# A graph network of two layers on one core: a channel kept as a row, and loads, a sum and a product moved to later places in their queues

## The chip, the core and the metric

The kernel runs on one core of a Trainium2 chip. A core has a matrix engine (TensorE, PE in the profile), a vector engine (VectorE, DVE), a scalar engine (ScalarE, ACT), a general engine (GpSimd, POOL) and a synchronising engine (SyncE, SP) that here only issues DMAs. Each engine works through its own queue in order and waits on semaphores for the others. The metric is the device time of one execution in microseconds; the median of three runs before the change is 2042.75 us (2042.57 to 2043.82).

## What is computed

64 graphs of N = 256 nodes with D = 256 channels go through two layers, all in fp32. Cut to what matters:

```python
# layer 0
h = einsum(d^-1/2 A d^-1/2 + alpha I, x)      # A: adjacency, d: degrees
x = layernorm(x + h @ W.T + b)                # this x is called x1 in the kernel
# layer 1
h = relu(bn1(conv1(x)))                       # 1 tap
x_conv = relu(bn2(conv2(h)) + x)              # 17 taps along the nodes, 256 x 256 channels
s = x @ w_se.T + b_se                         # 3 numbers a node
A = exp(-|s_n - s_m|^2);  msg = relu(x @ w_msg.T + b_msg);  x_nmp = A @ msg
out = GRU(input=[x_conv, x_nmp], state=x)     # w_ih (3D x 2D), w_hh (3D x D)
x = layernorm(x + out)
```

## The kernel before

**Rounds.** The 64 graphs go in NQ = 4 rounds of Q = 16. For each graph, `layer0` makes x1 and stores it to DRAM (L461); `layer1` transposes it (`x1_transposed`, L464), runs conv1 (L487), the messages (L508), a transform of h along the nodes (L526) into the tile V, the distances and their exponentials (L550, L551), the weighing by the adjacency (L554) and the aggregation (L563), and stores the transposed x1 and x_nmp to DRAM as xn_d (L568). The 17-tap convolution is done for a whole round at once: products of V with transformed weights u (`products`, L611, loads of u on SP at L581, six tiles deep), then an inverse transform on DVE (`complex_end`, L787) which stores to DRAM as xc_d.

**Gates.** The GRU of a graph (`gru`, L914) follows a round later. It is done as seven products instead of eight by a Strassen-like scheme: p1 to p7, each three matmuls (six records in the profile) of 128 x 384, with sums of blocks of the input made on POOL (`input_sums`, L893, line L901) and sums of weights in the tile wall made once in the first round (`gate_weights`, L1156). The first four gates of a round (EARLY = 4) are spread among the last graphs of the next round; the other twelve run beside the next round's products; the sixteen gates of the last round run alone at the end. `in_blocks(g)` is true for the first four of each round and all of the last: 28 graphs.

**Early gates' input.** For these 28, x_conv's argument is loaded in blocks (L830), transposed on DVE (L872, or L874 in the last round), x1 is added to it on POOL (L875), and two ReLUs on ACT follow (L879). Layer 1 folds the biases into the matmuls through channel 0: `x1_transposed` writes a constant 1 in place of it (L471, with `unit` and `others_only`), so the transposed tile lacks channel 0 of x1. That channel is loaded apart, as a column of x1_d with 256 elements of 4 bytes each (L844), into a tile of one partition, and added to partition 0 on POOL (L876); one is taken off again in the ReLU's bias (`less_one`).

**Queues and order.** The code is a set of generators; each `yield` is a place where another one may go on, and `graphs` (L1083), `merge`, `take` and `paced` say in what order they are written. That order is a priority only: a scheduler then goes through each engine's work, and takes a later instruction first where an earlier one is not ready by its own estimate of times. What must not move ahead is held by `with tc.issue_after(i):`, which puts what the block holds behind instruction `i` in the same engine's queue, without a wait. In the first round, `others` (L1193) gives each graph i one part of the transformed weights: `weights(setup, i, scale2)` (L316), 13 parts with matmuls, a difference on DVE (L339), a sum on POOL (L340) and three stores issued by POOL (L342); the graphs 13 to 15 have the gate weights' steps instead. `load_x` and `load_adj` (L108, L104) fetch the graph three ahead, on SP. `load_gate`, `load_conv` and `load_x1` (L838, L823, L846) fetch a gate's data, on SP too.

In a gate, the order of the products is this (a is the part of the input, b the part of wall):

```python
        p1 = product(A11, B11)          # evicted to `first` by ACT, L941
        p7 = product(S[3], T3)
        ...
        p6 = product(S[2], T2)          # the sixth product
        mark(nc.vector.tensor_add(quarter(0, 1), first, p6), 1)          # L947
        nc.vector.tensor_add(quarter(1, 1), quarter(0, 1), p7)           # L948
        product(A12, B21, p1)
        ...
        p5 = product(S[1], T1)
        ...
        product(A22, T4, p7)            # onto p7, so behind L948
        ...
        product(S[4], B22, p5)
```

The products lie in four banks of PSUM. After them come tanh (L977, L993), the mixing on DVE (L983 to L995) and the last layernorm (L353 to L364, with a power on POOL at L356).

Of the kernel before, what the change touches and what calls it, by code (L numbers as in the profile page):

```python
# [26 lines left out]
def kernel(  # L27
# [79 lines left out]

    def load_x(g):  # L108
        xin[g] = loads.tile([P, NCH, D], F32, name="x_t")
        nc.sync.dma_start(xin[g], x[g].rearrange("(c p) f -> p c f", p=P))  # L110

    def load(g):
        if g < B:
# [9 lines left out]

    vectors = const.tile([16, P], F32, name="bn_in")
    unused = const.tile([P, N], F32, name="unused")
    neg_half = const.tile([P, 4], F32)
    nc.vector.memset(neg_half, -0.5)
    load(0)
# [241 lines left out]

    xc_d = [dram.tile([Q, N, D], F32, name=f"xc_d{q}") for q in range(NQ)]
    x1_d = [dram.tile([Q, N, D], F32, name=f"x1_d{q}") for q in range(NQ)]
    xn_d = [dram.tile([P, 2 * DCH, N], F32, name=f"xn_d{g}") for g in range(B)]
    XN = {}
    ALONE = set()
    EXP, WEIGHED, NORMED = {}, {}, []
    gate = None
    EAGER = {0, Q - 4, Q - 3, Q - 2, *range(Q, Q + 13), 2 * Q + 5, 2 * Q + 6, 3 * Q + 5, 3 * Q + 6}
# [85 lines left out]
    def x1_transposed(g):  # L464
        x1 = X1.pop(g)
        xn = XN[g] = work.tile([P, 2 * DCH, N], F32, name="xn")
        p = bank("p_x1T").rearrange("p (k n) -> p k n", k=DCH)
        for k in range(DCH):
            for c in range(NCH):
                nc.tensor.transpose(p[:, k, c * P : (c + 1) * P], x1[:, c, k * P : (k + 1) * P], ident)  # L470
        nc.scalar.activation(xn[:, 0], p[:, 0], AF.Identity, bias=unit, scale=others_only)  # L471
        nc.scalar.copy(xn[:, 2 * DCH - 1], p[:, 1])

    def layer1(g, place):

# [8 lines left out]
        for c in range(NCH):  # L484
            p = bank("p_conv1")[:, : D + NSE]
            for k in range(DCH):
                nc.tensor.matmul(  # L487
                    p, x1T[:, k, c * P : (c + 1) * P], wc1[:, k, :], start=k == 0, stop=k == DCH - 1
                )
# [86 lines left out]

    TILES, AWAY = [V], []

    def load_u(n, i):
        u = ustream.tile([P, DCH, D], F32, name="u")  # L580
        nc.sync.dma_start(  # L581
            u, ud[i][n * GC : (n + 1) * GC].rearrange("c g o -> (c g) o")[:D].rearrange("(p k) o -> p k o", k=DCH)
        )
        return u

    def product(p, j, v, u, onto=False):
# [227 lines left out]

    GATE, CONV, SUMS, OWN, CHANNEL = {}, {}, {}, {}, {}


    EARLY = 4

    def in_blocks(g):  # L820
        return g % Q < EARLY or g >= B - Q

    def load_conv(g):  # L823
        y = xc_d[g // Q][g % Q]
        if in_blocks(g):


            CONV[g] = gate.tile([P, DCH, N // RB, RB], F32, name="xc_blocks", tag="xc_g")
            for b in range(NB):
                nc.sync.dma_start(  # L830
                    CONV[g][b * RB : (b + 1) * RB],
                    y.rearrange("(s r) (k b j) -> b r k s j", r=RB, k=DCH, j=RB)[b],
                )
            return
        CONV[g] = gate.tile([P, NCH, D], F32, name="xc_g")
        nc.sync.dma_start(CONV[g], y.rearrange("(c p) d -> p c d", p=P))

    def load_gate(g):  # L838
        inputs = GATE[g] = gate.tile([P, 3 * DCH, N], F32, name="inputs")
        nc.sync.dma_start(inputs[:, : 2 * DCH], xn_d[g])  # L840
        if in_blocks(g):
            CHANNEL[g] = gate.tile([1, N], F32, name="channel", bufs=1)
            with nc.allow_non_contiguous_dma("one channel"):
                nc.sync.dma_start(CHANNEL[g], x1_d[g // Q][g % Q][:, 0:1].rearrange("n d -> d n"))  # L844

    def load_x1(g):  # L846
        OWN[g] = gate.tile([P, NCH, D], F32, name="x1_g")
        nc.sync.dma_start(OWN[g], x1_d[g // Q][g % Q].rearrange("(c p) d -> p c d", p=P))

    def sent(g):  # L850

# [12 lines left out]
    def transposed(g):  # L864

        inputs = GATE[g]
        xcT = inputs[:, 2 * DCH :]
        if in_blocks(g):
            to = xcT.rearrange("p k (s r) -> p k s r", r=RB)
            if g < B - Q:  # L870
                with tc.issue_after(WEIGHED[max(WEIGHED)]):
                    nc.vector.transpose(to, CONV.pop(g))  # L872
            else:
                behind(nc.vector.transpose(to, CONV.pop(g)))  # L874
            nc.gpsimd.tensor_tensor(xcT, xcT, inputs[:, 0 : 2 * DCH : 2 * DCH - 1], op=ALU.add)  # L875
            JOINED.append(nc.gpsimd.tensor_tensor(xcT[0:1, 0], xcT[0:1, 0], CHANNEL.pop(g), op=ALU.add).ins)  # L876
            with tc.issue_after(EXP[max(EXP)]):
                for k in range(DCH):
                    nc.scalar.activation(xcT[:, k], xcT[:, k], AF.Relu, bias=less_one[:, k : k + 1])  # L879
# [34 lines left out]
    def gru(g):  # L914
# [33 lines left out]
        nc.vector.tensor_add(quarter(1, 1), quarter(0, 1), p7)  # L948
        product(A12, B21, p1)
# [84 lines left out]
    def chain(*stages):  # L1034
        for stage in stages:
            yield from stage
# [37 lines left out]
    PLACES = (("other",), ("layer0",), ("layer0",), (), ("layer0",), ("other", "layer0"), ())  # L1074
    STATS, APPLIED = len(PLACES) - 1, 1
    ENDS = [iter(())]

    def of_layer0(g):
        if g not in LAYER0:
# [3 lines left out]
    def graphs(first, part, others):  # L1083


        for i in part:
# [7 lines left out]
            for piece, _ in enumerate(layer1(first + i, i)):  # L1094
                if piece == APPLIED:
                    with tc.issue_after(EVICTED[first + i]):
                        run(ENDS.pop())
                    ENDS.append(given["layer0"])
                elif piece == STATS:
                    next(given["layer0"], "end")  # L1100
                    next(of_layer0(first + i + 3), "end")
                    next(given["layer0"], "end")
                if AWAY and TILES[0] is V:
                    g = first + i
                    if g >= 2 * Q:
                        if piece == 5:
                            bring(g, nc.scalar.copy, 1, EXP[g])
                    elif piece == 2:
                        bring(g, nc.vector.tensor_copy, 4, DIAGONAL[g + 2])
                    elif piece == 5:  # L1110
                        bring(g, nc.scalar.copy, 3, EXP[g])
                        bring(g, nc.vector.tensor_copy, 5, WEIGHED[g])
                yield
                for name in PLACES[piece]:
                    if next(given[name], "end") != "end":
                        yield
                if piece == 0 and not first:
                    with tc.issue_after(TAPS_OF["last"]):
                        load_x(i + 3)
            yield from given["other"]  # L1120

    with tc.tile_pool(name="setup", bufs=1) as setup:
# [30 lines left out]
        without_first(wmsg, top[:, D + NSE :], nc.gpsimd)  # L1153
        nc.gpsimd.tensor_copy(wmsg[0:1, 0], biases[:, NSE:])

        def gate_weights():  # L1156
            for b, i, h in ((B11, 0, 0), (T1, 0, 1), (B21, 1, 0), (B22, 1, 1)):
                at = slice(h * HD, (h + 1) * HD)
                own = w_hhT[i * P : (i + 1) * P].rearrange("p (t d) -> p t d", t=3)
                nc.sync.dma_start(wall[:, b, 0, 0:1], own[:, 2:3, at])  # L1160
                nc.sync.dma_start(wall[:, b, 0, 1:3], own[:, 0:2, at])
                for k in range(DCH):
                    row = (D if i == 0 else 0) + k * P
                    nc.sync.dma_start(
                        wall[:, b, 1 + k], w_ihT[row : row + P].rearrange("p (t d) -> p t d", t=3)[:, :, at]
                    )
            nc.gpsimd.tensor_copy(less_one, bn2_bias)
            nc.gpsimd.tensor_tensor(less_one[:, 0:1], less_one[:, 0:1], unit, op=ALU.subtract)
            top = setup.tile([P, 3, 2, HD], F32, name="hh_top", tag="taps", bufs=2)
# [185 lines left out]
```

## Time and profile before

| | us |
|---|---|
| median of three runs | 2042.75 |
| profiled execution, whole | 2048.04 |
| its span | 2046.3 |
| VectorE busy in it | 1396.4 |
| ScalarE busy in it | 964.7 |
| GpSimd busy in it | 698.1 |
| mean clock granted to TensorE | 0.994 |

The profile is one execution, taken with the hardware profiler. A row of a timeline gives the start from the beginning of the span, the duration, the engine, the line of the kernel, the operation, the tiles (written <- read) and the shapes; in brackets stands how long the engine had been idle before it and what ended that wait. Matmuls are pipelined: a record of 128 x 384 is 0.49 us long, but the next one starts 0.32 us after it, so a bracket of 0.2 hides another 0.17. A row of the chain of waits gives start, duration and what the end of the execution was waiting for at that time. SPq and ACTq rows are issues of DMAs; their duration is that of the issue, not of the transfer. DMA engines are busy 33.8% of the span for SP's queue, 9.3% for ACT's and 6.3% for POOL's.

The first round takes the span up to about 256 us, its products come then; the products of the later rounds begin near 600, 1089 and 1571 us, and the last sixteen gates run alone from about 1800 us on.

### The profile page before, as it was taken

To read this page: it belongs to the slowest core of one execution; us is meant where nothing else is said; L and a number is where in the kernel's file an instruction comes from. 1 tells how busy PE (TensorE), PEld (TensorE's weight loads), DVE (VectorE), ACT (ScalarE), POOL (GpSimd) and SP (SyncE) were. 2 spreads that over 40 slices of the span, in tenths; PEclk is the share of its full clock that TensorE was granted. 3 is DMA by queue.
4 is the path that set the end of the run, shared out by engine and by line. 5 is a ranking of instruction groups with operands and counts; after the bars stand their busy time and mean duration, and the time that the engine had idled before them with its cause. 6 is when DMAs were issued, how large, how long until landed. Compare 5 with 4: busy or idle time off the path is not lost. (4 is left out here: it accounts for less than half of the span.)

```text
span 2046.3 us, 26391 instructions
## 1 busy us (share of the span) xinstructions
PE 1984.9 (97%) x8157; PEld 1437.7 (70%) x8157; DVE 1396.4 (68%) x3199; ACT 964.7 (47%) x2285; POOL 698.1 (34%) x679
## 2 busy tenths in 40 slices
PE   7999999999999999999999999999999999999997
PEld 6878788878667766777777766777777855555554
DVE  6334447787567788764546888874445899877787
ACT  5666654567442234566653233556664233333333
POOL 4444411232532143223322234322331045445543
PEclk8999999999999999999999999999999999999999
DMA  4766557544555654343336665334344745443431
GB/s 133 221 202 207 182 193 240 169 140 135 138 149 192 212 126 134 115 129 109 103 109 185 211 170 134 119 117 125 97 116 142 259 124 135 127 100 87 102 87 54
DMA packets 269021, 298.05 MB, mean 146 GB/s; under 512 B 84276, under 2 KB 211336, under 8 KB 268882
## 3 DMA queue, kind: packets, MB, share of 16 engines
q1 hardware_dynamic: 208842, 200.37, 33.8%
q10 hardware_dynamic: 44472, 67.39, 9.3%
q0 software_dynamic: 15568, 28.62, 6.3%
q8 instruction: 66, 1.08, 0.2%
q14 instruction: 73, 0.60, 0.1%
HBM read 193.19 MB, written 103.06 MB: 145 GB/s over the span
## 5 line engine op out<-in xcount | busy, mean ns | idle before, releaser
L930 PE MATMUL p_g<-wall,sums 128*128 128x384 f32 x1536 | 534.0, 488 | 6.1 <-POOL sums L901 3.2
L930 PEld LDWEIGHTS p_g<-wall,sums 128*128 128x128 f32 x1536 | 284.8, 190 | 193.4 <-issue 9.6
L930 PE MATMUL p_g<-wall,inputs 128*128 128x384 f32 x1152 | 406.8, 489 | 12.2 <-DVE G L948 12.2
L930 PEld LDWEIGHTS p_g<-wall,inputs 128*128 128x128 f32 x1152 | 215.3, 190 | 167.2 <-DVE G L948 27.8
L356 POOL TENSOR_TENSOR ln_rs<-ln_rs,neg_half 128x2 f32<-128x2 f32 x129 | 95.2, 738 | 546.7 <-DVE ln_rs L355 411.0
L901 POOL TENSOR_TENSOR sums<-inputs 128x384 f32<-128x384 f32 x128 | 143.1, 1118 | 329.0 <-PE p_g L930 303.2
L554 DVE TENSOR_TENSOR aT<-aT,adjT 128x512 f32<-128x512 f32 x64 | 45.2, 706 | 200.5 <-ACT aT L551 200.4
L435 POOL TENSOR_TENSOR x_t<-x_t,b_t 128x512 f32<-128x512 f32 x64 | 101.9, 1592 | 215.3 <-ACT x L432 138.8
L589 PE MATMUL p_k<-u,VM 128*128 128x256 f32 x736 | 169.6, 380 | 2.8 <-DMA u<-ud 1.6
L589 PEld LDWEIGHTS p_k<-u,VM 128*128 128x128 f32 x736 | 138.5, 190 | 25.6 <-PE p_k L589 2.5
L364 ACT ACTIVATE x_g<-x_g,ln_mr,ln_rs 128x256 f32<-128x256 f32 x128 | 70.0, 593 | 169.4 <-DVE ln_mr L360 164.6
L977 ACT ACTIVATE G<-G 128x512 f32<-128x512 f32 (+1 forms) x129 | 81.0, 628 | 128.7 <-DVE G L1004 91.9
L440 PE MATMUL p_hT<-adjT,x 128*128 128x256 f32 x512 | 125.7, 389 | 5.8 <-ACT x L432 2.3
L487 PE MATMUL p_conv<-wc,xn 128*128 128x259 f32 x512 | 126.5, 389 | 4.2 <-ACT xn L471 3.5
L563 PE MATMUL p_nmp<-aT,msg 128*128 128x256 f32 x512 | 121.4, 380 | 2.2 <-DVE aT L554 2.2
L450 PE MATMUL p_out<-w,hT 128*128 128x256 f32 x512 | 121.5, 380 | 0.9 <-ACT hT L445 0.7
L901 POOL TENSOR_TENSOR sums<-inputs,sums 128x384 f32<-128x384 f32 x64 | 74.8, 1169 | 138.0 <-PE p_g L930 137.9
L508 PE MATMUL p_msg<-wmsg,xn 128*128 128x256 f32 x512 | 121.9, 381 | 0.0
L487 PEld LDWEIGHTS p_conv<-wc,xn 128*128 128x128 f32 x512 | 99.1, 194 | 27.1 <-ACT xn L471 4.3
L526 PE MATMUL p_dft<-fwd,h 128*128 128x240 f32 x512 | 114.1, 366 | 0.0
L950 ACT COPY G<-p_g 128x512 f32<-128x512 f32 x64 | 37.4, 584 | 155.9 <-PE p_g L930 107.2
L450 PEld LDWEIGHTS p_out<-w,hT 128*128 128x128 f32 x512 | 95.6, 190 | 21.2 <-ACT hT L445 2.9
(173 smaller groups left out, 3596.9 us busy)
## 6 DMA issues: line engine op xcount, KB each, us to landing
u<-ud SPq DMA_DIRECT2D x284, 256.0 KB
xn_d<-xn ACTq DMA_DIRECT2D x64, 512.0 KB
inputs<-xn_d SPq DMA_DIRECT2D x64, 512.0 KB
ud<-u_set POOLq DMA_DIRECT2D x39, 480.0 KB, 6.3
adj_t<-in_adj_dram SPq DMA_DIRECT2D x64, 256.0 KB
x_t<-in_x_dram SPq DMA_DIRECT2D x64, 256.0 KB
x_d<-x ACTq DMA_DIRECT2D x64, 256.0 KB
xc_d<-VM SPq DMA_DIRECT2D x64, 256.0 KB
```

The costliest lines, as they stand in the source:

```text
L356: nc.gpsimd.tensor_tensor(rs[:, : len(chunks)], rs[:, : len(chunks)], neg_half[:, : len(chunks)], op=ALU.pow)
L435: nc.gpsimd.tensor_tensor(x_t, x_t, b0_t.unsqueeze(1).to_broadcast([P, NCH, D]), op=ALU.add)
L440: nc.tensor.matmul(p[:, k, :], x1[:, mc, k * P : (k + 1) * P], adjT[:, mc, 1 - mc : 3 - mc, :].rearrange("p n q -> p (n q)"), start=mc == ...
L450: nc.tensor.matmul(p[:, c, :], hT[:, k, c * P : (c + 1) * P], w0[:, k, :], start=k == 0, stop=k == DCH - 1)
L487: nc.tensor.matmul(p, x1T[:, k, c * P : (c + 1) * P], wc1[:, k, :], start=k == 0, stop=k == DCH - 1)
L508: nc.tensor.matmul(p[:, c, :], x1T[:, k, c * P : (c + 1) * P], wmsg[:, k, :], start=k == 0, stop=k == DCH - 1)
L526: nc.tensor.matmul(p[:, t0 * FL : t1 * FL], h[:, c, k * P : (k + 1) * P], fwd[:, first : first + t1 - t0, :].rearrange("p t f -> p (t f)") ...
L563: nc.tensor.matmul(p[:, k, :], msg[:, mc, k * P : (k + 1) * P], aT[:, mc].rearrange("p n q -> p (n q)"), start=mc == 0, stop=mc == NCH - 1,)
L589: nc.tensor.matmul(p[:, j * D : (j + 1) * D], v[:, k, :], u[:, k, :], start=k == 0 and j == 0 and not onto, stop=k == DCH - 1, skip_group_ ...
L901: nc.gpsimd.tensor_tensor(S[i], x, y, op=op)
L930: nc.tensor.matmul(p[:, : 3 * HD] if k == 0 else p[:, HD:], a[:, k], wall[:, b, k].rearrange("p t d -> p (t d)"), start=first and k == 0, ...
L977: nc.scalar.activation(rz, rz, AF.Tanh, scale=0.5)
```

## The change

The diff has six parts.

1. The 28 graphs of `in_blocks` get their channel 0 as a row: `x1_transposed` copies it from PSUM into row 64 of a tile of which rows 0 to 63 are the old dist_l (ACT), and stores it to DRAM (on ACT's queue for the first round, on SP's later). `load_gate` loads this row of 1 KB instead of the column. The addition of it goes from POOL, behind L875, to DVE, ahead of L875.
2. The sixteen loads of gate weights leave `gate_weights` for a generator of their own, two steps of which are taken in each graph from the fourth on, each behind the last load of x.
3. The last part of the transformed weights does its sum, difference and stores one graph later, and the first step of `gate_weights` follows it.
4. `load_conv`, `load_gate` (without the channel) and `load_x1` are put behind the last load of u written so far.
5. The sixth product of an early gate (not of the last round) is put behind the last conv1 written so far.
6. What these need is noted: `xin["last"]`, `LAST_U`, `CONV1`.

```diff
+            xin["last"] = nc.sync.dma_start(xin[g], x[g].rearrange("(c p) f -> p c f", p=P)).ins
...
+    both_rows = const.tile([P, N], F32, name="dist_l")
+    dl, channel = both_rows[0:64], both_rows[64:65]
...
+    channel_d = [dram.tile([1, N], F32, name=f"channel_d{g}") for g in range(B)]
...
         nc.scalar.copy(xn[:, 2 * DCH - 1], p[:, 1])
+        if in_blocks(g):
+            nc.scalar.copy(channel, p[0:1, 0])
+            (nc.scalar if g < Q else nc.sync).dma_start(channel_d[g], channel)
...
-                nc.tensor.matmul(
+                CONV1[g] = nc.tensor.matmul(
                     p, x1T[:, k, c * P : (c + 1) * P], wc1[:, k, :], start=k == 0, stop=k == DCH - 1
-                )
+                ).ins
...
-        dl = work.tile([64, N], F32, name="dist_l", bufs=1)
         nc.scalar.copy(dl, p[0:64, :N])
...
+    def behind_u():
+        return tc.issue_after(LAST_U[0])
...
     def load_gate(g):
         inputs = GATE[g] = gate.tile([P, 3 * DCH, N], F32, name="inputs")
-        nc.sync.dma_start(inputs[:, : 2 * DCH], xn_d[g])
+        with behind_u():
+            nc.sync.dma_start(inputs[:, : 2 * DCH], xn_d[g])
         if in_blocks(g):
             CHANNEL[g] = gate.tile([1, N], F32, name="channel", bufs=1)
-            with nc.allow_non_contiguous_dma("one channel"):
-                nc.sync.dma_start(CHANNEL[g], x1_d[g // Q][g % Q][:, 0:1].rearrange("n d -> d n"))
+            nc.sync.dma_start(CHANNEL[g], channel_d[g])

     def load_x1(g):
         OWN[g] = gate.tile([P, NCH, D], F32, name="x1_g")
-        nc.sync.dma_start(OWN[g], x1_d[g // Q][g % Q].rearrange("(c p) d -> p c d", p=P))
+        with behind_u():
+            nc.sync.dma_start(OWN[g], x1_d[g // Q][g % Q].rearrange("(c p) d -> p c d", p=P))
...
-            nc.gpsimd.tensor_tensor(xcT, xcT, inputs[:, 0 : 2 * DCH : 2 * DCH - 1], op=ALU.add)
-            JOINED.append(nc.gpsimd.tensor_tensor(xcT[0:1, 0], xcT[0:1, 0], CHANNEL.pop(g), op=ALU.add).ins)
+            nc.vector.tensor_add(xcT[0:1, 0], xcT[0:1, 0], CHANNEL.pop(g))
+            JOINED.append(nc.gpsimd.tensor_tensor(xcT, xcT, inputs[:, 0 : 2 * DCH : 2 * DCH - 1], op=ALU.add).ins)
...
-        p6 = product(S[2], T2)
+        with tc.issue_after(CONV1[max(CONV1)]) if in_blocks(g) and g < B - Q else ExitStack():
+            p6 = product(S[2], T2)
...
+                if piece == 3 and not first and i >= 3:
+                    next(beside["loads"], "end")
+                    next(beside["loads"], "end")
...
-        def gate_weights():
+        def gate_loads():
             for b, i, h in ((B11, 0, 0), (T1, 0, 1), (B21, 1, 0), (B22, 1, 1)):
...
+                for to, what in pairs:
+                    with tc.issue_after(xin["last"]):
+                        nc.sync.dma_start(to, what)
+                    yield
...
-        more_weights = gate_weights()
+        more_weights, beside["loads"] = gate_weights(), gate_loads()
         others = [weights(setup, i, scale2) for i in range(NPARTS)]
         others[0] = later(others[0])
-        others += [take(more_weights, i) for i in (1, 3, 2)]
+        last = others.pop()
+        others += [take(last, 2), chain(later(last), take(more_weights, 1)), take(more_weights, 3), take(more_weights, 2)]
```

More of the change, by code (lines that the diff above doesn't have):

```diff
@@ L109, in load_x @@
         xin[g] = loads.tile([P, NCH, D], F32, name="x_t")
-        nc.sync.dma_start(xin[g], x[g].rearrange("(c p) f -> p c f", p=P))
+        xin["last"] = nc.sync.dma_start(xin[g], x[g].rearrange("(c p) f -> p c f", p=P)).ins
     def load(g):
@@ L375, with in_blocks @@
     ALONE = set()
+    EARLY = 4
+    def in_blocks(g):
+        return g % Q < EARLY or g >= B - Q
+    CONV1 = {}
     EXP, WEIGHED, NORMED = {}, {}, []
@@ L577 @@
     TILES, AWAY = [V], []
+    LAST_U = {}
+    def behind_u():
+        return tc.issue_after(LAST_U[0])
     def load_u(n, i):
         u = ustream.tile([P, DCH, D], F32, name="u")
-        nc.sync.dma_start(
+        LAST_U[0] = nc.sync.dma_start(
             u, ud[i][n * GC : (n + 1) * GC].rearrange("c g o -> (c g) o")[:D].rearrange("(p k) o -> p k o", k=DCH)
-        )
+        ).ins
         return u
@@ L815 @@
     GATE, CONV, SUMS, OWN, CHANNEL = {}, {}, {}, {}, {}
-    EARLY = 4
-    def in_blocks(g):
-        return g % Q < EARLY or g >= B - Q
     def load_conv(g):
@@ L828, in load_conv @@
             CONV[g] = gate.tile([P, DCH, N // RB, RB], F32, name="xc_blocks", tag="xc_g")
[L829 to L833, printed above, removed]
+            with behind_u():
+                for b in range(NB):
+                    nc.sync.dma_start(
+                        CONV[g][b * RB : (b + 1) * RB],
+                        y.rearrange("(s r) (k b j) -> b r k s j", r=RB, k=DCH, j=RB)[b],
+                    )
             return
         CONV[g] = gate.tile([P, NCH, D], F32, name="xc_g")
-        nc.sync.dma_start(CONV[g], y.rearrange("(c p) d -> p c d", p=P))
+        with behind_u():
+            nc.sync.dma_start(CONV[g], y.rearrange("(c p) d -> p c d", p=P))
     def load_gate(g):
         inputs = GATE[g] = gate.tile([P, 3 * DCH, N], F32, name="inputs")
-        nc.sync.dma_start(inputs[:, : 2 * DCH], xn_d[g])
+        with behind_u():
+            nc.sync.dma_start(inputs[:, : 2 * DCH], xn_d[g])
         if in_blocks(g):
             CHANNEL[g] = gate.tile([1, N], F32, name="channel", bufs=1)
-            with nc.allow_non_contiguous_dma("one channel"):
-                nc.sync.dma_start(CHANNEL[g], x1_d[g // Q][g % Q][:, 0:1].rearrange("n d -> d n"))
+            nc.sync.dma_start(CHANNEL[g], channel_d[g])
     def load_x1(g):
         OWN[g] = gate.tile([P, NCH, D], F32, name="x1_g")
-        nc.sync.dma_start(OWN[g], x1_d[g // Q][g % Q].rearrange("(c p) d -> p c d", p=P))
+        with behind_u():
+            nc.sync.dma_start(OWN[g], x1_d[g // Q][g % Q].rearrange("(c p) d -> p c d", p=P))
     def sent(g):
@@ L1076 @@
     ENDS = [iter(())]
+    beside = {}
     def of_layer0(g):
@@ L1159, in gate_weights @@
                 own = w_hhT[i * P : (i + 1) * P].rearrange("p (t d) -> p t d", t=3)
-                nc.sync.dma_start(wall[:, b, 0, 0:1], own[:, 2:3, at])
-                nc.sync.dma_start(wall[:, b, 0, 1:3], own[:, 0:2, at])
+                pairs = [(wall[:, b, 0, 0:1], own[:, 2:3, at]), (wall[:, b, 0, 1:3], own[:, 0:2, at])]
                 for k in range(DCH):
                     row = (D if i == 0 else 0) + k * P
-                    nc.sync.dma_start(
-                        wall[:, b, 1 + k], w_ihT[row : row + P].rearrange("p (t d) -> p t d", t=3)[:, :, at]
-                    )
+                    pairs.append((wall[:, b, 1 + k], w_ihT[row : row + P].rearrange("p (t d) -> p t d", t=3)[:, :, at]))
+                for to, what in pairs:
+                    with tc.issue_after(xin["last"]):
+                        nc.sync.dma_start(to, what)
+                    yield
+        def gate_weights():
             nc.gpsimd.tensor_copy(less_one, bn2_bias)
```

## The prediction

> **What bounds the kernel now.** I read the page's busy shares first, then TensorE's waits, then the timeline around the longest of them and the chain of waits in the last stage. TensorE (PE) is busy 1984.9 of 2046.3 us, so 61.4 us is all that any reordering can touch.
>
> ```profile
> PE 1984.9 (97%) x8157; PEld 1437.7 (70%) x8157; DVE 1396.4 (68%) x3199; ACT 964.7 (47%) x2285; POOL 698.1 (34%) x679
> ```
>
> The windows by stage split the 61.4: 11.7 idle in 0 to 26 us, 5.8 in 26 to 256, 20.2 in 256 to 1640, 8.7 in 1640 to 1806, 4.3 in 1806 to 2018, 10.8 at the tail. The first and the last lie before the first transpose and behind the last product, and the change has no part there. Between them are about 39 us. The edits meet five places; these are PE's own stalls, number in brackets:
>
> ```profile
> 113.33 2.96 PE L487 MATMUL p_conv<-wc,xn 128*128 128x259 f32 x6 [3.52 <-ACT xn L471]
> ...
> 245.95 2.61 PE L440 MATMUL p_hT<-adjT,x 128*128 128x256 f32 x6 [1.67 <-DVE adjT L417]
> ...
> 605.13 1.13 PE L589 MATMUL p_k<-u,ab 128*128 128x256 f32 x4 [1.25 <-DMA u<-ud]
> ...
> 1428.13 2.20 PE L930 MATMUL p_g<-wall,sums 128*128 128x384 f32 x6 [1.62 <-POOL sums L901]
> ...
> 1848.26 2.20 PE L930 MATMUL p_g<-wall,inputs 128*128 128x384 f32 x6 [0.21 <-DVE G L948]
> ```
>
> **Gate weights' loads, two per graph.** Written in graph 13, they are issued as early as 34 us, in groups of up to six, because nothing orders them behind anything. At 111.93 us ACT's store of xn was issued; ACT had stood still before it, and the row names the transfer:
>
> ```profile
> 112.32 0.42 ACT L393 ACTIVATE adjT<-adj_t 128x256 f32<-128x256 f32 x1 [4.93 <-DMA wall<-in_w_hhT_dram]
> ```
>
> L471, which conv1 needs, stood behind it: PE lost 3.52. In the change at most two such loads lie behind each x load, over graphs 3 to 10, where before five or six did. Their 16 issues (0.5 to 3.3 us each while the queue is backed up) stay on SP, ahead of the next adjacency load; that one goes out at 227.00 and is first read at 237.85, so some 4 us of issuing are covered. If that cover fails, a graph loses what 113 lost. Ends: -3.5 to +3.5; I take **-3.5**, as loads in groups of five at 65 to 73 us already passed without a stall.
>
> **Last spectra sum.** L339 (1.21), L340 (2.97) and three DMA issues (1.63 on POOL) of part 12 run at 239.35. DVE's L497 then takes 2.32 (0.17 a graph before) and L417 2.69 (0.62): both end as a POOL instruction ends (242.78, 245.64). PE loses 0.57 + 1.67 = 2.24. One graph later they follow L554, with L455 and the layernorm of DVE behind them and L356 behind on POOL; POOL's 4.6 us there may delay L356, whose result is needed by ACT about 2 us later. The sum has no new order edge, so it can also be issued early again. Ends -2.2 and +2; I take half the gain, **-1.1**.
>
> **Gates' loads behind u.** At 605 the reason is an x1 load of a gate three product steps later in the program, at the head of SP's queue, waiting for an output store:
>
> ```profile
> 601.77 0.36 SPq L848 DMA_DIRECT2D x_g<-x_d  x1
> 602.22 8.47 SPq L581 DMA_DIRECT2D u<-ud  x11
> ```
>
> A u slot was free at about 600.4 (end of p_real). Behind u the x1 load no longer blocks: 1.25 + 0.15 go, **-1.4**. The later stalls on u (0.55 at 642, 0.88 and 0.18 at 1094, 0.69 at 1131) have other rows ahead (an x_t load at 1089.16, products in between), and the same bytes still pass: 0, ends -1.2 to +1.2. The gates' inputs come some 8 us later in this stage; a gate needs about 36 us there (x1 loads at 601.77 and 638.38), which covers it. At 1590 to 1640 u passes without a stall.
>
> **Sixth product.** It matters only in the first gate of a round (939 and 1428, 1.62 each), where it was put ahead of conv1; in later gates p6 already follows the distances. But conv1's input ends at 1427.70 + 0.36 = 1428.06, only 0.07 sooner than p6 started. ACT was held by the ReLUs that wait for POOL. There L876 (0.72) goes, while DVE's add (0.41 by L1183, the same 1x256) comes ahead of L875: about 0.1 sooner. So 2 x 0.17, taken as **-0.3**, not 3.2. Ends -3.2 to +1 (what then waits: L947, L948 and the bank of p6, with four banks).
>
> **Channel as a row.** Per early gate (28) it removes L876 from POOL and a load of 256 elements from SP; adds a 1x256 add on DVE, a 1x256 copy on ACT, a 1 KB store (24 on SP, 4 on ACT). [...] What counts is L876, in the last stage's loop:
>
> ```profile
> 1836.47 4.38 DMA inputs<-xn_d
> ...
> 1840.98 1.43 POOL inputs L875
> 1842.41 0.07 issue
> 1842.48 1.06 POOL inputs L876
> 1843.56 0.51 ACT inputs L879
> 1844.07 0.53 ACT G L993
> 1844.62 0.70 DVE G L994
> ...
> 1848.26 1.88 PE p_g L930 x5
> ```
>
> The inputs' slot comes free with PE's product, and the chain leads back to PE: 14.03 us, where 42 matmul records at 0.3225 (twelve in 3.87) need 13.55. Fifteen periods from 1806.20 to 2017.86 take 211.66, so 8.5 us over the floor. Without L876 both ReLUs follow L875 at once: ACT at 1842.43, then two more operations at 0.42 to 0.49, so tanh L993 at about 1843.76 instead of 1843.98: 0.22 per period, and 0.48 (all) if the copy L941 falls behind it. In three long periods (14.4 to 14.5) DVE's L989 takes 2.17 instead of 0.68, until L876 and the L901 behind it are done:
>
> ```profile
> 1940.36 1.05 POOL L876 TENSOR_TENSOR inputs<-inputs,channel 1x256 f32<-1x256 f32 x1
> 1940.76 2.17 DVE L989 SCALAR_TENSOR_TENSOR G<-G 128x512 f32<-128x512 f32 x1
> 1941.38 0.99 POOL L901 TENSOR_TENSOR sums<-inputs 128x384 f32<-128x384 f32 x1
> ```
>
> [...] If each of the 16 hit a L901, that would be 16 x 1.0 us on DVE; by the rows POOL is idle from 1837.09 to 1838.52, just when the transpose ends (1837.79), and DVE is idle 0.62 there: 0.41 fits, cost 0. L901 merely moves up by 1.05, and L989 ends that much sooner, about 0.98 down to the floor. Sum: 12 x 0.22 + 3 x 0.98 = **-5.5**, ends 0 and -8.5.
>
> ACT's 28 copies (L472 takes 0.36) lie ahead of L490 or L567, before which ACT idles (1.94 and 1.14 at 27 and 225 us); without that cover 28 x 0.3 = 8. SP's 24 stores wait for ACT with adj, x or u loads queued behind, six u slots being 5.2 us of work. ACT's four stores could stand as at 112 (4.9 once). For all this **+0.6**, ends 0 and 5. The shared tile costs nothing: ACT writes both rows in order, and the store has several us before the next write.
>
> Sum on the profiled execution (2048.04 with what lies around its 2046.3 span): -3.5 - 1.1 - 1.4 - 0.3 - 5.5 + 0.6 = -11.2. The median is 2042.75, 5.3 below that execution; the stalls are the same schedule's, so I subtract there: **2031.6 us**.
>
> **Rivals.** *The time goes elsewhere, 2041.* Two thirds of the gain fails: the wall loads delay some other graph as much, and tanh stays where it is because the copy and both ReLUs run ahead of it and the sums take DVE's time. For it: 14.03 is within 0.5 of the floor, L989 is still slowed by L875, and the orders inside the queues are made anew. Against it: the 3.5 has one named cause. Only the 1.4 and crumbs stay.
>
> *Slower: DVE waits for the channel row.* The new add stands right behind the transpose, with L1004, L986 and the rest of the gate behind it. Before, the channel's load left SP at 1843.92, and 0.54 + 3.3 (a 1 KB row to biases lands in 3.3) puts it 3 us ahead of the next transpose. If SP places it behind the next inputs load (1850.49), it lands at 1854.7; the transpose ends near 1851.8, DVE stands 2.9, less its 0.62, so L989 ends 2.3 later and tanh 1.3: 15 x 1.3 = 19.5, less 5.7 of the other edits: **2056.6**. It decides once the row lands over 0.8 us behind the transpose. Against it: the slot now frees with the DVE add, 5 us earlier than with L876.
>
> *Everything fits, 2023.* All of the last stage (8.5), 2.2, 3.2 for p6 and 3.5 + 1.4, and a stall on u.
>
> **Numbers.** A difference under 0.2% (4.1 us) can't be told from none. Forecast with its neighbourhood 0.62, everything fits 0.10, elsewhere 0.16, slower 0.12. So faster 0.72, same 0.16, slower 0.12. The range 2023 to 2043 leaves out the slower case and little below; the likeliest case's own is 2026 to 2038.
>
> **What would show it.** No stall at 113 and 605; periods near 13.7 in the last stage with no POOL row between L875 and the ReLUs; conv1 ahead of p6 but a stall of over a us still there, now on xn. Wrong would be: DVE idle before the channel add, wall loads again in groups, the sum of part 12 still at 239, or new ACT idle behind a channel store.

## The result and the profile after

| | before | after |
|---|---|---|
| median, first comparison (4 runs each) | 2043.28 us | 2027.07 us |
| median, second comparison (12 and 5 runs) | 2041.88 us | 2028.73 us |
| profiled execution, whole | 2048.04 us | 2026.31 us |
| its span | 2046.3 us | 2024.5 us |

The ratio is 0.9921 [0.9904, 0.9938] in the first comparison and 0.9932 [0.9919, 0.9945] in the second: 16.2 and 13.2 us less. The forecast was 11.2 less. The two profiled executions differ by 21.7 us, more than the medians do; the reason is told below.

The busy times of the changed kernel, first line of its page:

```profile
PE 1978.0 (98%) x8157; PEld 1437.5 (71%) x8157; DVE 1401.3 (69%) x3227; ACT 971.7 (48%) x2313; POOL 679.4 (34%) x651
```

The counts show the channel part of the edit: 28 instructions fewer on POOL, 28 more on DVE, 28 more on ACT. TensorE's count is the same and its busy time is 6.9 us shorter, so what went was not idle time alone: some matmuls of the execution before were slow (the eight records of conv1 behind the 3.52 at 113 took 3.59 us, in the trace after 1.92). The prediction's 61.4 us of idle time were therefore not all that could go.

The next rows are from the timeline of after, at the places that the prediction named. First the neighbourhood of 113 us. Two weight loads pass behind one x load, and conv1 takes its usual 1.92 for eight records with no stall:

```profile
106.43 4.44 SPq L1184 DMA_DIRECT2D wall<-in_w_hhT_dram  x2
...
108.98 1.92 PE L499 MATMUL p_conv<-wc,xn 128*128 128x259 f32 x8
```

Then the last spectra sum. Both stalls are where they were: 0.56 at 237 (0.57 before), and 1.66 here (1.67 before):

```profile
239.92 1.53 PE L449 MATMUL p_hT<-adjT,x 128*128 128x256 f32 x6 [1.66 <-DVE adjT L426]
```

The first products of the second round, where the prediction had the 1.25 at 605: the SP queue has u ahead of the gates' loads, and the product at 604 starts with no wait for u:

```profile
595.63 0.38 SPq L853 DMA_DIRECT2D inputs<-xn_d  x1
596.11 10.21 SPq L597 DMA_DIRECT2D u<-ud  x8
...
604.08 1.89 PE L605 MATMUL p_k<-u,ab 128*128 128x256 f32 x8
```

The first early gate in the fourth round, where p6 had waited 1.62 at 1428. The row with wall,inputs between p7 and conv1 is the product A12·B21, which in the program's text comes after p6:

```profile
1410.98 1.46 PE L943 MATMUL p_g<-wall,sums 128*128 128x384 f32 x4
1412.27 2.10 PE L943 MATMUL p_g<-wall,inputs 128*128 128x384 f32 x6
1413.67 0.36 ACT L481 COPY xn<-p_x1T 128x256 f32<-128x256 f32 x1
...
1414.20 1.91 PE L499 MATMUL p_conv<-wc,xn 128*128 128x259 f32 x8
```

Last a period of the final stage. DVE adds the channel behind its transpose without standing still, no POOL row lies between L889 (L875 before) and the ReLUs, and ACT goes through ReLU, copy, ReLU and tanh with no wait after the first:

```profile
1834.64 0.70 DVE L887 STREAM_TRANSPOSE inputs<-xc_blocks 128x512 f32<-128x512 f32 x1
1835.38 0.41 DVE L888 TENSOR_TENSOR inputs<-inputs,channel 1x256 f32<-1x256 f32 x1
...
1838.29 1.67 POOL L889 TENSOR_TENSOR inputs<-inputs 128x512 f32<-128x512 f32 x1 [1.21 <-DVE G L997]
...
1839.99 0.51 ACT L892 ACTIVATE inputs<-inputs,less_one 128x256 f32<-128x256 f32 x1 [2.67 <-POOL inputs L889]
1840.41 0.57 ACT L954 COPY first<-p_g 128x512 f32<-128x512 f32 x1
1840.87 0.51 ACT L892 ACTIVATE inputs<-inputs,less_one 128x256 f32<-128x256 f32 x1
1841.29 0.62 ACT L1007 ACTIVATE G<-G 128x512 f32<-128x512 f32 x1
```

Where the chain of waits had led through the inputs' load and POOL before, it is now TensorE alone from 1824.76 on, 45.49 us in one piece:

```profile
1824.76 45.49 PE p_g L943 x139
```

The windows of after for 1806.20 to 2000.00 show TensorE busy for 193.80 of 193.80 us (before, 207.35 of the 211.66 from 1806.20 to 2017.86). The starts of the sixteen gates lie 13.77 apart (10 of 15) or 13.55 (5), in sum 6.2 less than before (14.02, and three times 14.4 to 14.5).

### The profile page after: what moved, and what is told of

Its sections match the earlier page's. It is cut to its first block, busy times and chain, and to the rows that moved or that the text cites. A ratio compares the mean times of both kernels' runs of the same rounds, so it can differ in the third digit from the quotient of the medians.

```text
span 2024.5 us, 26452 instructions
## 1 busy us (share of the span) xinstructions
PE 1978.0 (98%) x8157; PEld 1437.5 (71%) x8157; DVE 1401.3 (69%) x3227; ACT 971.7 (48%) x2313; POOL 679.4 (34%) x651
## 2 busy tenths in 40 slices
DMA packets 261518, 298.09 MB, mean 147 GB/s; under 512 B 76716, under 2 KB 203832, under 8 KB 261378
## 5 line engine op out<-in xcount | busy, mean ns | idle before, releaser
L914 POOL TENSOR_TENSOR sums<-inputs 128x384 f32<-128x384 f32 x128 | 150.4, 1175 | 256.1 <-PE p_g L943 226.3
L449 PEld LDWEIGHTS p_hT<-adjT,x 128*128 128x128 f32 x512 | 93.2, 193 | 25.7 <-ACT x L441 9.9
```

Source lines behind the costliest of these rows:

```text
L449: nc.tensor.matmul(p[:, k, :], x1[:, mc, k * P : (k + 1) * P], adjT[:, mc, 1 - mc : 3 - mc, :].rearrange("p n q -> p (n q)"), start=mc == ...
L914: nc.gpsimd.tensor_tensor(S[i], x, y, op=op)
```

## The experiments

The theory after this result: the parts are independent, and the forecast missed because some of its terms were wrong in opposite directions. The rival: a term works only together with others. The first four kernels each take one part of the change alone into the kernel before. Beside the medians I compare starts of the same matmul in two traces, stage by stage; "+1.87" is what a kernel gains on another in such a stretch. Each trace is one execution, so such a difference counts only where the edit can reach. The median of before was 2041.97 (33 runs) beside the first four kernels, 2041.66 (24) beside the second four and 2041.88 (12) beside the last.

**The last spectra sum alone (sum_only).**

```diff
-        others += [take(more_weights, i) for i in (1, 3, 2)]
+        last = others.pop()
+        others += [take(last, 2), chain(later(last), take(more_weights, 1)), take(more_weights, 3), take(more_weights, 2)]
```

> The kernel before with only the last spectra sum moved one graph later in the program. All five engines' orders of instructions come out the same as before, so the theory 'the edit is void' expects 2043 us (within 1 us), the stalls of 0.57 and 1.67 at 243 and 246 us unchanged, and it serves as a second look at the kernel before: it shows whether the half-speed matmuls behind 246 us come again. The prediction's half gain (-1.1 us through another place of the sum) is the rival: 2042 and no stall there.

Measured: 2042.16 us, ratio 1.0006 [0.9997, 1.0015]. The compiled order of instructions, which is what the scheduler made of the text, is the same as that of the kernel before on all five engines, and that of the changed kernel without this edit is the same as with it. The text was moved, the scheduler put the sum where it had been: this part of the change does nothing. That makes this kernel's trace a second trace of the program before. It has the 0.57 and 1.67 of 240 us, but not the stall of 3.52 at 113; stage by stage the trace shown before loses 5.35 on it at that place, and 1.60 behind the stall at 246, where its matmuls are slow (six records in 2.61 us against 1.53; the clock, in the last section).

**The gate weights' loads alone (wall_only).**

```diff
+                if piece == 3 and not first and i >= 3:
+                    next(beside["loads"], "end")
+                    next(beside["loads"], "end")
...
+                    with tc.issue_after(xin["last"]):
+                        nc.sync.dma_start(to, what)
+                    yield
```

> The kernel before with only the gate weights' loads two per graph. Theory: it takes away the stall of 3.52 us at 113 and the half clock that follows it (eight conv1 matmuls in 3.59 instead of 1.92), so the first round ends some 5.3 us sooner: 2038 us, if the runs without a profile have that stall too. Rival (the prediction's sum): 3.5 us only, 2039.8. If the profile itself makes that stall larger, less than 3 us: above 2040.

Measured: 2041.60 us, 0.9999 [0.9990, 1.0008]. Nothing, and the orders on TensorE, DVE and ACT are unchanged. The 3.52 at 113 is missing here, but it is missing too in sum_only, p6_only, u_only, column_dve, row_pool and p6_both, which all issue these loads as before. (channel_only has 0.68 at 95.) So the size of the stall in the profile before was a chance of that one execution.

The wait behind it is not. ACT's store of xn uses no weights; but in the trace before, the store at 111.93 signals its end on the same semaphore as the weight load issued at 99.63, and ACT waits for that semaphore first (4.93 in the row at 112.32). The same pairing stands in the seven traces named, at about 91 and 107 us. Six of them, all but sum_only, show ACT waiting for a weight load there, 0.60 to 2.10 us, mostly without TensorE noticing. In wall_only, and in the changed kernel, the semaphore's former user is a store of ACT's own, and no such wait is left.

**p6 behind conv1 alone (p6_only).**

```diff
-        p6 = product(S[2], T2)
+        with tc.issue_after(CONV1[max(CONV1)]) if in_blocks(g) and g < B - Q else ExitStack():
+            p6 = product(S[2], T2)
```

> The kernel before with only the sixth product behind conv1. In the orders of the engines TensorE has A12 B21 where p6 stood, twice. Theory: A12 B21 does not need POOL's sums and fills the wait, so each of the two stalls of 1.62 (1.89 with what the pipelining hides) goes without any of the channel edit: -3.8, 2039.5 us. Rival (the prediction): conv1 is the only one to come ahead, and its input is no sooner: -0.3, 2043 us, with a stall of over a us on xn.

Measured: 2038.16 us, 0.9986 [0.9977, 0.9995], 3.8 less. Stage by stage against sum_only: +1.87 in the stretch around 939 and +1.87 in the one around 1428. Elsewhere it differs only by what varies between executions; at 600 us it even loses 1.7, at stalls on u. On TensorE exactly two things change places, twice: p6 and A12·B21. Timeline of p6_only, the same place as above:

```profile
1417.19 2.10 PE L931 MATMUL p_g<-wall,inputs 128*128 128x384 f32 x6
...
1418.54 0.36 ACT L473 COPY xn<-p_x1T 128x256 f32<-128x256 f32 x1
1419.13 1.91 PE L488 MATMUL p_conv<-wc,xn 128*128 128x259 f32 x8
```

The xn copy ends at 1418.90, while A12·B21 runs until about 1419.13. conv1's input is still late, but a product lies in the hole.

**The gates' loads behind u alone (u_only).**

```diff
-        nc.sync.dma_start(CONV[g], y.rearrange("(c p) d -> p c d", p=P))
+        with behind_u():
+            nc.sync.dma_start(CONV[g], y.rearrange("(c p) d -> p c d", p=P))
```

and the same around the loads of the inputs, the blocks and x1.

> The kernel before with only the gates' loads behind the loads of u. Theory: all stalls on u that had an x1 load or an inputs load among the u loads go: 1.25 and 0.15 at 605, 0.55 at 642, 0.69 at 1131, some 4 us with what the pipelining hides: 2039.3 us; the one at 1094, behind an x_t load, stays at 0.9. Rival (the prediction): only the one at 605 goes, 1.4: 2041.9, and those at 642 and 1131 stay.

Measured: 2038.36 us, 0.9985 [0.9976, 0.9994], 3.6 less. Against sum_only its trace gains 2.90 in the products of the second round, 0.63 in the third's, and about 1.5 behind that, of which no part is traced to the edit. In sum_only the x1 load stands in front of u, as in the profile before:

```profile
593.56 0.36 SPq L848 DMA_DIRECT2D x_g<-x_d  x1
594.01 8.81 SPq L581 DMA_DIRECT2D u<-ud  x11
...
597.42 1.13 PE L589 MATMUL p_k<-u,ab 128*128 128x256 f32 x4 [1.94 <-DMA u<-ud]
```

These stalls vary between executions. The first one is 1.25 in the profile before and 1.32 to 1.94 in the eight other traces in which these loads are not held back. The next product waits too in some: 0.15 in the profile before, 0.51 in wall_only, 0.68 in p6_only, 1.40 in row_pool. A later one, 0.55 at 642 in the profile before, also has an x1 load in front:

```profile
638.38 0.42 SPq L848 DMA_DIRECT2D x_g<-x_d  x1
...
642.37 3.69 PE L589 MATMUL p_k<-u,VM 128*128 128x256 f32 x16 [0.55 <-DMA u<-ud]
```

With the loads behind u all of these are gone.

The second four ask what in the channel part pays, and whether A12·B21 is the reason for p6's gain.

**The whole channel part alone (channel_only)**, all of part 1 of the change: its edits to `x1_transposed`, `load_gate` and the addition.

> The kernel before with only the channel's part: copied from PSUM and stored as a row, loaded as a row, added by DVE ahead of L875. Theory: it carries the whole gain of the last sixteen gates, periods of 13.77 or 13.55 instead of 14.02 to 14.53, and nothing elsewhere: -6.3, 2037 us; the stalls at 939 and 1428 stay near 1.6. Rival: the channel part also helps the first gates of the rounds (POOL has 0.72 less there) and gives 2035.

Measured: 2035.18 us, 0.9966 [0.9953, 0.9978], 6.5 less. The last sixteen gates gain 5.23 on sum_only; their period is 13.77.

**Only the addition on DVE, the column load kept (column_dve).**

```diff
-            nc.gpsimd.tensor_tensor(xcT, xcT, inputs[:, 0 : 2 * DCH : 2 * DCH - 1], op=ALU.add)
-            JOINED.append(nc.gpsimd.tensor_tensor(xcT[0:1, 0], xcT[0:1, 0], CHANNEL.pop(g), op=ALU.add).ins)
+            nc.vector.tensor_add(xcT[0:1, 0], xcT[0:1, 0], CHANNEL.pop(g))
+            JOINED.append(nc.gpsimd.tensor_tensor(xcT, xcT, inputs[:, 0 : 2 * DCH : 2 * DCH - 1], op=ALU.add).ins)
```

> The kernel before with the addition of the channel on DVE ahead of L875, but loaded as a column of 256 elements as before (no row, no copy, no store). Theory (what counts is the instruction that leaves POOL's part of the loop, the descriptors are hidden): as much as the whole channel part, 2037 us, periods of 13.77. Rival (the descriptors count): no better than 2041, since the row is not there.

Measured: 2036.85 us, 0.9977 [0.9966, 0.9987], 4.8 less, with 4.80 gained in the last gates and the same period of 13.77. In its timeline the slot comes free with the DVE addition, so that the column's load has some 10 us to land before the next addition at 1857.48:

```profile
1843.71 0.41 DVE L875 TENSOR_TENSOR inputs<-inputs,channel 1x256 f32<-1x256 f32 x1
...
1847.65 0.55 SPq L844 DMA_DIRECT2D channel<-x_d  x1
```

**Only the row, the addition left on POOL (row_pool)**: channel_only with its last hunk, the one shown for column_dve, undone.

> The kernel before with the row copied, stored and loaded, but added on POOL behind L875 as before. Theory: 0, 2043 us within 1 us, periods of 14.0 to 14.5 as before, ACT busy some 7 us longer and hidden. Rival (the descriptors count): 2040 or better. Rival (the copies and stores cost): 2045 or worse.

Measured: 2044.61 us, 1.0012 [1.0001, 1.0022], 2.9 more. The period stays at 14.02, and the reason is in its timeline, ReLU L882 behind POOL's addition:

```profile
1841.65 0.51 ACT L882 ACTIVATE inputs<-inputs,less_one 128x256 f32<-128x256 f32 x1 [2.66 <-POOL inputs L878]
1841.69 1.06 POOL L879 TENSOR_TENSOR inputs<-inputs,channel 1x256 f32<-1x256 f32 x1
...
1842.79 0.51 ACT L882 ACTIVATE inputs<-inputs,less_one 128x256 f32<-128x256 f32 x1 [0.15 <-POOL inputs L879]
```

So the addition's move carries the gain. The row by itself gains nothing; whether it costs is open: the interval only just leaves 1, and the places where this trace loses on sum_only are 3.3 us at the u stalls of the second round, most of it in slow matmuls behind them (15 records of p_k in 6.14 us, against 16 in 3.69 in sum_only), and 3.3 us at one wait for DVE, with slow matmuls behind it too (both in the last section). Neither lies beside the new ACT copies or stores. With the addition on DVE the row is 1.7 us ahead of the column, less than the two intervals tell apart.

**p6 and A12·B21 both behind conv1 (p6_both).**

```diff
         with tc.issue_after(CONV1[max(CONV1)]) if in_blocks(g) and g < B - Q else ExitStack():
             p6 = product(S[2], T2)
...
-        product(A12, B21, p1)
+        with tc.issue_after(CONV1[max(CONV1)]) if in_blocks(g) and g < B - Q else ExitStack():
+            product(A12, B21, p1)
```

> The kernel before with both the sixth product and A12 B21 put behind conv1. If A12 B21 is what fills the wait, the gain is lost here: TensorE waits for conv1's input instead, a stall of about 1.5 us named after xn at 939 and at 1428, 2043 us within 1 us. If moving p6 alone is what helps, 2039.5 as with p6 alone.

Measured: 2040.44 us, 0.9996 [0.9987, 1.0005]. Against sum_only each of the two places gains 0.26 in the end, where the forecast had 0.17. The stall that it predicted is there, on xn:

```profile
1418.94 2.02 PE L488 MATMUL p_conv<-wc,xn 128*128 128x259 f32 x8 [1.34 <-ACT xn L472]
```

This settles p6: the gain is A12·B21 in the hole, not conv1 in it.

The last four run beside each other, two of them on what was left: does a group of weight loads cost anything, and what is the sum worth if it really moves?

**The changed kernel again (after_again)**, as their common measure.

> The changed kernel as it is, beside the three kernels of this call. Theory (its parts are worth 3.7, 3.6 and 6.5 us and the two others nothing): 14 us less than the kernel before on the same chip. Rival (the loads of the gate weights are worth 2 to 3 us once the other parts are in): 16 to 17 less. Expected: ratio 0.992 to 0.9935.

Measured: 2028.73 us, 0.9932 [0.9919, 0.9945], 13.2 less than before. The parts alone give 14.1 by their medians (3.8 + 3.6 + 6.5 + 0.4 for wall_only - 0.2 for sum_only) and 11.9 by their ratios, against 16.2 and 13.2 for the whole, with 11.2 to 16.5 in this comparison's interval. Terms that need each other aren't called for, though a surplus of a few us can't be excluded.

**The changed kernel without the spreading of the weight loads (after_nowall)**, part 2 undone.

> The changed kernel without the spreading of the gate weights' loads: they are issued as in the kernel before. Theory (the spreading is worth nothing): within 0.5 us of the changed kernel in the median, no stall at 113 us, or one in some executions only. Rival (it saves the 3.5 us stall on conv1's input of the fifth or sixth graph in each execution): 3 to 4 us more than the changed kernel.

Measured: 2028.28 us, 0.9934 [0.9921, 0.9947]: 0.4 less than after_again, so no worth beside the other parts either.

**All sixteen weight loads at once, in the fifth graph (wall_burst)**, on the kernel before.

```diff
+                if piece == 3 and not first and i == 4:
+                    for _ in range(16):
+                        next(beside["loads"], "end")
```

> The kernel before, with its sixteen loads of gate weights all issued in one go in the fifth graph, where they are spread over many graphs in the kernel before and two per graph in the change. Theory (these loads can hold up ACT's store, but seldom, and TensorE then loses 3.5 us in one place): within 2 us of the kernel before, at most one graph with a stall. Rival (grouped loads of gate weights are what costs, so a bigger group costs more): a stall of over 3.5 us on conv1's input in the graphs that follow, 3 to 8 us more than the kernel before.

Measured: 2048.74 us, 1.0029 [1.0016, 1.0041], 6.9 more. My theory falls. The rival holds in size, not in form: the stall on conv1's input is 2.18, not over 3.5, and comes in one graph, not several. There the stall of the profile before comes back, with ACT's store again behind a weight load of the same semaphore (issued at 107.82) and conv1 behind that. The first rows are the timeline; the windows below give, for each stretch, its length, the busy times, the granted clock (1.00 is full speed), the DMA share and GB/s:

```profile
110.94 0.42 ACT L393 ACTIVATE adjT<-adj_t 128x256 f32<-128x256 f32 x1 [3.60 <-DMA wall<-in_w_hhT_dram]
...
111.95 2.82 PE L487 MATMUL p_conv<-wc,xn 128*128 128x259 f32 x8 [2.18 <-ACT xn L471]
```

```profile
110.00:113.00 3.00, 1.05 (x5) 0.94 (x6) 1.49 (x4) 2.06 (x6) 1.28 (x2) 1.00 0.97 307
113.00:116.00 3.00, 3.00 (x11) 2.42 (x10) 0.62 (x4) 2.25 (x8) 3.00 (x3) 0.50 0.95 270
```

The stall is 2.18, and TensorE's granted clock is 0.50 from 113 to 116: conv1, the transposes and the messages take 2.82, 1.06 and 2.39 instead of 1.92, 0.60 and 1.89. In this stage its trace loses 4.1 us on sum_only, as the kernel before's own trace lost 5.35 there. It loses 1.2 more in the next graph, where a load of taps, queued on SP behind the burst, comes late and TensorE stands 0.98. Another 1.6 go at 246, as in the profile before, and 2.3 in the last gates, which this edit doesn't touch. So a group of sixteen brings about what groups of up to six did only by chance.

**The changed kernel with the last spectra sum really held (sum_behind).**

```diff
-        with tc.issue_after(ADEG[n + 3]), tc.issue_after(POWERS[n + 3]):
+        final = n + 1 == NPARTS
+        with tc.issue_after(DIAGONAL[n + 3] if final else ADEG[n + 3]), tc.issue_after(X_BIASED[n + 3] if final else POWERS[n + 3]):
...
-            nc.gpsimd.tensor_tensor(x_t, x_t, b0_t.unsqueeze(1).to_broadcast([P, NCH, D]), op=ALU.add)
+            X_BIASED[g] = nc.gpsimd.tensor_tensor(x_t, x_t, b0_t.unsqueeze(1).to_broadcast([P, NCH, D]), op=ALU.add).ins
```

> The changed kernel, with the last spectra sum really held back: its difference L339 on DVE behind the last graph's scaled diagonal, its sum L340 on POOL behind the last graph's bias add. Theory (the sum at 237 to 240 makes TensorE wait 0.56 + 1.66 us there): both stalls go, 1 to 2.2 us less than the changed kernel; up to 3.8 less where a clock drop followed the stall. Rival (the sum only moves the stall, since the last graph needs POOL and DVE as well): no difference, with a stall of 1 to 2 us some 13 us later.

Measured: 2025.86 us (2025.51 to 2026.89), 0.9919 [0.9907, 0.9932], below every run of after_again (2026.93 to 2029.97); the means differ by 2.5, while the two intervals against the kernel before overlap. Both stalls are gone. What stands 13 us later is no new one: after_again has it as well (0.82 at 252):

```profile
236.26 1.89 PE L450 MATMUL p_hT<-adjT,x 128*128 128x256 f32 x8
...
249.67 1.99 PE L450 MATMUL p_hT<-adjT,x 128*128 128x256 f32 x8 [0.81 <-ACT x L442]
```

Stage by stage it gains 2.6 on after_again at the two stalls and keeps that for some 450 us. Its one trace gives it back later, 0.6 at a u stall of 1.03 and 1.6 in two gate periods of 14.37; the runs say that this isn't the rule. Its median is the lowest here.

## Why the prediction was right, and where its steps failed

The direction, the range and the main term were right: the kernel gained at three of the five places that were named, most of all from POOL's addition leaving the last stage. The size was 11.2 against 16.2 and 13.2, and that nearness is partly luck: two terms forecast 4.6 us that did not come, and the other three were too small by some 7 us.

- **Gate weights' loads, -3.5 forecast, 0 measured.** The step that failed is "at 111.93 us ACT's store of xn was issued; ACT had stood still before it", where the whole 3.52 behind it was read as a property of the schedule. That ACT waits there is one, since the store shares its semaphore with a weight load; how long it waits is not. Eight other traces with the loads issued as before (after_nowall is the eighth) show TensorE losing 0 or 0.68 to it, and the median of before (2041.7 to 2043.3) doesn't contain it. A sign lay in the table: the profiled execution took 2048.04, 5.3 above the median, and in the stage comparison this stall and the slow matmuls behind it are 5.35 (the slow matmuls at 246 add 1.60). I noted the 5.3 and subtracted a gain of that execution from the median all the same. A larger group of loads brings the loss into the median (wall_burst); the groups of the kernel before don't.
- **Last spectra sum, -1.1 forecast, 0 measured.** The prediction said that the sum could also be issued early again, and it was. Half of 2.24 was a mean of two cases, of which one had to come true. The other case is worth 2.5 to 2.9 (sum_behind), since the two stalls go entirely; the feared delay of L356 did not show.
- **Gates' loads behind u, -1.4 forecast, -3.6 measured.** Right mechanism, mis-sized term. The stalls at 642 (0.55) and 1131 (0.69) were put at 0 because other rows stood ahead of their loads of u. That was misread: an x1 load stands ahead of them in the trace before as well, at 638.38 and at 1127.56, and with the loads behind u both stalls go. The stall that was counted varies, and its 1.25 was the smallest of nine traces (up to 1.94). The stall that stays, 0.89 at 1081, is one behind an x_t load, as the prediction had it.
- **Sixth product, -0.3 forecast, -3.8 measured.** The failed step is that conv1's input ends "only 0.07 sooner than p6 started": true in kind, as p6_both shows with its 0.26 per place, but it asks only what conv1 can do with p6's place. The product that came next in the program, A12·B21, needed nothing that was late. With p6 held it moved up and covered the wait: 2 x 1.87.
- **Channel as a row, -5.5 forecast, with +0.6 for copies and stores; -6.5 measured.** L876's leaving is worth what was worked out: the sixteen gates' starts 6.2 us closer, 0.25 per usual period (0.22 forecast), no long periods left, and ACT in the order that was assumed. In five periods of 15 the floor of 13.55 is reached. The row itself against the column is worth under 2 us. In the trace before, the column's load is issued in 0.52 to 0.58 us and no engine is listed as waiting for it; the trace after has 7560 fewer packets under 512 bytes (76716 against 84276). The feared collision of the DVE addition with POOL (L989 took 2.17 instead of 0.68 beside L876 and L901 in the trace before) did not come up: all 28 additions take 0.41 in the trace after. POOL's L889 takes up to 1.77 in the last gates, against 1.27 at best, and TensorE does not wait for it. The 0.6 is not told apart from 0: row_pool's loss can't be put down to it.

Of the rivals, that DVE waits for the channel row had its answer in column_dve and channel_only: in the last gates the load is issued 8 to 10 us before it is read. That all fits (2023) came true for p6 and u, not for the sum; sum_behind at 2025.9 is close to it.

## What to carry to other kernels

Before a stall in one profile is priced, compare the profiled execution with the median: if it is slower by about the size of the stall, the stall may be that execution's alone. When an instruction that waits is held back, look past the one it makes way for, to the next in the program that needs nothing late. When an engine waits for a transfer whose data it does not use, look for a semaphore that the two share. And when a statement is moved under a scheduler that orders by its own estimates, compare the compiled orders first, for the move may be void. A small operation between a producer and the engine that everybody waits for (here 1.06 us on POOL for 256 numbers) is worth moving to an engine with a hole at that time, whatever the data's shape.

## What the runs showed of the hardware

Behind some stalls of these runs TensorE's granted clock fell to about half (0.50 to 0.54), behind others of the same length it did not. Where the clock was read, it is the mean of the stretch in brackets; the stall of row_pool at 1264 is this one:

```profile
1264.57 3.86 PE L933 MATMUL p_g<-wall,sums 128*128 128x384 f32 x6 [1.99 <-DVE G L961]
```

| trace, stall in us | granted clock | TensorE's records behind the stall |
|---|---|---|
| before, 3.52 at 113 | 0.52 (113 to 116) | eight of conv1 in 3.59 us, 1.92 in the trace after |
| before, 1.67 at 246 | 0.54 (246 to 249) | six of p_hT in 2.61, 1.53 in the trace after |
| wall_burst, 2.18 at 112 | 0.50 (113 to 116) | eight of conv1 in 2.82 |
| row_pool, 1.99 at 1264 | 0.91 (1262 to 1282) | six of p_g in 3.86, 2.10 at 1258 |
| row_pool, 1.53 at 597 and 1.40 behind it | not read | 15 of p_k in 6.14, 16 in 3.69 in sum_only |
| sum_only, 1.67 at 240 | 1.00 (120 to 256) | six of p_hT in 1.53 |
| sum_only, 1.94 at 597 | not read | 16 of p_k in 3.69 |
| after, 1.66 at 240 | 1.00 (240 to 243) | six of p_hT in 1.53 |
| after, 1.79 at 383 | 1.00 (383 to 386) | eight of p_nmp in 1.99 |

So the length of a stall alone does not tell: before and sum_only have the same compiled order and the same 1.67 there, and only one of them the slow records. What else decides is not shown here. The slow records cost 1.67 us at 113 (3.59 against 1.92), 1.60 at 246 by the comparison of stages, and 1.76 in row_pool (3.86 against 2.10). So in these traces one stall cost its own length in one execution and 1.6 us more in another. This is a source of differences between executions of one program here.
